# Edge counts kept as node by source tile: a bank evicted in one run, seven source tiles widened at once, eight gather buffers

## The chip, the core and the metric

The kernel runs on one core of one Trainium2 chip. Its engines work side by side, each through its own instructions in order, and wait for one another by semaphores: PE (TensorE, matrix products; its weight loads are shown as PEld), DVE (VectorE), ACT (ScalarE), POOL (GpSimd, which here issues the gathers and scatters) and SP (which issues plain DMAs). The metric is the device time of one execution in microseconds (us), the median of several runs.

## What is computed

One graph block over 6250 nodes with 256 features and 200,000 edges sorted by destination: a normalised input, a graph convolution plus a linear attention block, both added to the input, and then a mixture of 8 experts. The part that the change touches is the sum over edges in the graph convolution:

```python
edge_index = jnp.stack([src, dst])
xn = _layernorm(x, axis=-1)
x = x + gnn(edge_index, xn, W, b) + mix(xn, ...)
...
# in gnn, with self-loops appended to src and dst:
deg = segment_sum(ones, dst)
dinv = rsqrt(deg)
norm = dinv[src] * dinv[dst]
h = X @ W
out = relu(segment_sum(h[src] * norm[:, None], dst) + b)
```

The kernel sums the scaled rows of X over the edges of each node first, and multiplies by W behind it.

## The kernel before, in words

Nodes are handled in 49 tiles of 128 (`NB` = 49). The program has three stages. Up to about 273 us it searches the edge list, builds per-tile lists and scales the rows of X into `tab` (high and low part of each row side by side, 512 columns; all 49 tiles stay in SBUF as `source(t)` and are copied to `g_dram`). From 273 to about 1352 us runs the graph stage. Then the 8 experts run to the end.

**The graph stage** is three generators that are stepped in turn while the program is built (lines 1281 to 1302), so that each engine's order of instructions is fixed by that interleaving, under a manual schedule. One pass of the outer loop is one step of `gather`; `dense` is stepped as often as keeps it in proportion, `NGT + LAG` passes for `(ND + 1) * NS + 1` steps; `rounds` is stepped 1.25 times.

- **`gather`** (L971 to L998) serves 18 of the 49 destination tiles. Each of 612 passes issues an indirect DMA on POOL that fetches 128 rows of `g_dram` into a tile `gt` (L977), and, `LAG` = 7 passes later, multiplies the tile of seven passes ago by a one-hot matrix `oh` into PSUM (L995). `gt` has `GB` = 9 buffers.
- **`dense`** (L914 to L969) serves the other 31 destination tiles (`ND` = 31). For a destination tile `u` it builds a matrix of edge counts A and multiplies it with the source tiles. The 128 nodes are taken as 64 pairs, 5 pairs to a step, 13 steps (`NS` = 13, index `p`; the last step has 4 pairs). In a step DVE makes one-hot matrices `lo` (source row within its tile, 128 wide) and `hi` (98 wide: source tile and which node of the pair; L899); PE multiplies them pair by pair into one PSUM bank `bp` (L963), 98 columns for each pair; ACT copies the bank as bytes into `A` (L965). Before the change a pair's 98 columns are ordered by source tile, then node (`hi` = 2 x source tile + node, made at L592), and `A` lies as source tile by node, `[P, 49, 128]`. A bank of 10 nodes therefore goes to 245 places of `A`: 2 adjacent bytes, 128 bytes apart.
- The products with the source tiles come one destination tile later: while tile `u` is being counted, PE multiplies the counts of tile `u - 1`. Step `p` (1 to 12) takes 4 source tiles (the last one 5): `share(p)`. Before it, ACT widens those 4 slabs of bytes to 4-byte numbers in `A_r` (`widened`, L926, 512 elements per partition, or 640; 2 buffers); then PE does one 128x512 matmul per source tile into `ps_d` (L952). `make(k + 2)` lets DVE make the one-hots two steps ahead.
- **`rounds`** (L1083 to L1279) carries finished pairs of tiles on: attention, two layer norms, a two-layer MLP, gate and routing. It uses all engines; the lines that matter below are the normalisation on ACT from statistics of DVE (`nb` L1193, `s` and `slot` L1199), the transposes on PE that follow (L242), `agt` L1134, `x1t` L1213, `xmt` L1222, `ht` L1235 on ACT, the softmax of the routing with its ACT table load (L1025) and the scatter on POOL (L1076).

In one dense step the order is: PE's products L952 of step `p`; DVE's one-hots of step `p + 2`; ACT's widening for step `p + 1`; PE's counting L963; ACT's eviction L965. Since ACT works in order, a widening stands behind the eviction of the step before and behind whatever `rounds` put there.

Of the kernel before, what the change touches and what calls it, by code (L numbers as in the profile page):

```python
# [10 lines left out]
U8 = mybir.dt.uint8  # L11
FR = mybir.dt.float32r
AF = mybir.ActivationFunctionType
OP = mybir.AluOpType
# [4 lines left out]
P = 128  # L19
# [3 lines left out]
NB = 49  # L23
# [16 lines left out]
ND = len(DTS)  # L40
GN = 2
NG = P // GN
HI = NB * GN
NDC = (ND + 3) // 4
LS = 5
NS = (NG + LS - 1) // LS
# [2 lines left out]
NGT = NGB * EB  # L49
NGC = (NGT + P - 1) // P  # L50
IC = 64
GB = 9
LAG = 7
AHEAD = 4
SIDE = 1.25
NX = 6
# [13 lines left out]
def graph_block_kernel(  # L70
# [5 lines left out]
    nc = tc.nc  # L76
    V = nc.vector
# [39 lines left out]
    def table(t):  # L117

        k = t // 8
        if k not in tabs:  # L120
            where = (3, 4, 5, 0, 1, 2, 6)[k]
            tabs[k] = big.tile([P, min(8, NB - 8 * k), 2 * D], FR, name="tab", tag=f"T{where}")
            if k == NB // 8:
                V.tensor_copy(tabs[k][:, 0, :].rearrange("p (h d) -> p h d", h=2),
                              zeros.unsqueeze(1).to_broadcast([P, 2, D]))
        return tabs[k], t - 8 * k
# [5 lines left out]
    def source(t):  # L132
        o, at = table(t)
        return o[:, at, :]
# [368 lines left out]
    def edge_lists():  # L503
# [19 lines left out]
        for k, v in enumerate((begin_d, pid_d)):  # L523
            o = sm_ps[:, 128 + 32 * k:128 + 32 * k + 2 * NDC]
# [17 lines left out]
        def ask(c):  # L542
            if c < NGC:
                got[c] = [rw.tile([P, P], I32, name=o, tag=o) for o in ("gd", "gs")]
                fetch(got[c], gsi[:, c:c + 1])
            elif c < NGC + NDC:
                d = 2 * (c - NGC)
                got[c] = [rw.tile([P, 2, P], I32, name=o, tag=o) for o in ("wd", "ws")]
                for h in range(2):
                    fetch([w[:, h, :] for w in got[c]], ei[:, d + h:d + h + 1])  # L550
# [28 lines left out]
        for c in range(NDC):  # L579
            wd, ws = got.pop(NGC + c)  # L580
            hs = rw.tile([P, 2, P], I32, name="hs", tag="hs")
            kf = wd.bitcast(F32)
            for h in range(2):
                V.tensor_scalar(kf[:, h, :], wd[:, h, :], node0[:, 2 * c + h:2 * c + h + 1], None, op0=OP.subtract)
            vl = rw.tile([P, 2, P], F32, name="vl", tag="vl", bufs=1)
            V.tensor_scalar(vl, kf, 0.0, None, op0=OP.is_ge)
            V.scalar_tensor_tensor(vl, kf, float(GN), vl, op0=OP.is_lt, op1=OP.mult)
            V.tensor_copy(vend[:, 2 * c:2 * c + 2], vl[:, :, P - 1])
            yield
            V.tensor_scalar(hs, ws, 7, None, op0=OP.arith_shift_right)  # L590
            V.tensor_scalar(ws, ws, P - 1, None, op0=OP.bitwise_and)
            V.scalar_tensor_tensor(kf, hs, float(GN), kf, op0=OP.mult, op1=OP.add)  # L592
            yield
            V.scalar_tensor_tensor(kf, kf, -200.0, vl, op0=OP.add, op1=OP.mult)
            V.tensor_scalar(kf, kf, 200.0, None, op0=OP.add)
            lf = hs.bitcast(F32)
            V.tensor_copy(lf, ws)
            yield
            for v, o in ((kf, hiT), (lf, loT)):
                et_ps = rps.tile([P, 512], F32, name="et_ps", tag="et_ps", bufs=2)  # L600
                for h in range(2):
                    nc.tensor.transpose(et_ps[:, h * P:(h + 1) * P], v[:, h, :], ident)
                nc.scalar.copy(o[:, 4 * c:4 * c + 4, :].rearrange("p b g -> p (b g)"), et_ps[:, :2 * P])
            ask(NGC + c + 2)
            yield
# [264 lines left out]

    with tc.tile_pool(name="ga", bufs=GB, side="right") as ga, \
            tc.tile_pool(name="de", bufs=2, side="right") as de, \
# [9 lines left out]
        def put_sum(t, ps):  # L882
            gi = t // 2
            if gi not in sums:
                sums[gi] = pair("G", 3, "ag")
            V.tensor_reduce(sums[gi][:, t % 2, :], ps.rearrange("p (h d) -> p d h", h=2), AX.X, OP.add)
            there.add(t)

        def groups(p):
            return LS * p, min(NG, LS * (p + 1))  # L890

        def onehots(lists, p):

            o = []
            g0, g1 = groups(p)
            for name, row, w, t in (("lo", rowb, P, lists[0]), ("hi", hib, HI, lists[1])):
                one = de.tile([P, LS, w], BF16, name=name, tag=name, bufs=3)
                full = [P, g1 - g0, w // 2, 2]
                V.tensor_tensor(one[:, :g1 - g0, :].rearrange("p g (w t) -> p g w t", t=2),  # L899
                                row.rearrange("p (w t) -> p w t", t=2).unsqueeze(1).to_broadcast(full),  # L900
                                t[:, g0:g1, :].unsqueeze(2).to_broadcast(full), op=OP.is_equal)
                o.append(one)
            return o

        def twice(u):

            o = []
            for name, t in (("lo2", loT), ("hi2", hiT)):
                two = de.tile([P, NG, 2], BF16, name=name, tag=name)
                nc.scalar.copy(two, t[:, u, :].unsqueeze(2).to_broadcast([P, NG, 2]))  # L910
                o.append(two)
            return o

        def dense():  # L914

            mats, parts = {}, {}
            acc_ps = None

            def share(p):
                return (p - 1) * NB // (NS - 1), p * NB // (NS - 1)  # L920

            def widened(u, p):

                s0, s1 = share(p)
                o = parts[p] = de.tile([P, 5, P], FR, name="A_r", tag="A_r")
                nc.scalar.copy(o[:, :s1 - s0, :], mats[u][:, s0:s1, :])  # L926

            steps = [(u, p) for u in range(ND) for p in range(NS)]
            twos_ = {0: twice(0)}
            made = {}  # L930

            def make(k):
                if k < len(steps):
                    u, p = steps[k]
                    made[k] = onehots(twos_[u], p)
                    if p == NS // 2 and u + 1 < ND:
                        twos_[u + 1] = twice(u + 1)

            make(0)
            make(1)  # L940
            yield
            for u in range(ND + 1):
                for p in range(NS):
                    k = u * NS + p
                    if u >= 1 and p >= 1:

                        if p == 1:
                            acc_ps = dps.tile([P, 2 * D], F32, name="ps_d", tag="ps_d")
                            nc.tensor.matmul(acc_ps, identr, source(DTS[u - 1]), start=True, stop=False)
                        A, (s0, s1) = parts.pop(p), share(p)  # L950
                        for hi in range(s0, s1):
                            nc.tensor.matmul(acc_ps, A[:, hi - s0, :], source(hi), start=False, stop=(hi == NB - 1))  # L952
                    make(k + 2)
                    if u < ND and p == 0:
                        mats[u] = de.tile([P, NB, P], U8, name="A", tag="A")
                    if u >= 1 and p < NS - 1:
                        widened(u - 1, p + 1)
                    if u < ND:
                        lo, hi = made.pop(k)
                        g0, g1 = groups(p)  # L960
                        bp = bps.tile([P, 512], F32, name="bp", tag="bp")
                        for g in range(g1 - g0):
                            nc.tensor.matmul(bp[:, g * HI:(g + 1) * HI], lo[:, g, :], hi[:, g, :],  # L963
                                             start=(g == 0), stop=(g == g1 - g0 - 1))
                        nc.scalar.copy(mats[u][:, :, GN * g0:GN * g1].rearrange("p s (g k) -> p g s k", k=GN),  # L965
                                       bp[:, :(g1 - g0) * HI].rearrange("p (g s k) -> p g s k", g=g1 - g0, k=GN))
                    if u >= 1 and p == NS - 1:
                        put_sum(DTS[u - 1], acc_ps)
                    yield  # L969

        def gather():  # L971
            tiles, ohs = {}, {}
            ps = None
            for j in range(NGT + LAG):
                if j < NGT:
# [4 lines left out]
                    if j % IC == IC - 1:  # L980
                        sources(j // IC + 2)
                i = j - LAG
                m = i + AHEAD
# [310 lines left out]
        while any(alive.values()):  # L1294
            step("g", G)
            while alive["d"] and done_d * (NGT + LAG) < n_dense * (j + 1):
                step("d", Dn)
# [146 lines left out]
```

## Time and profile before

| | |
|---|---|
| median of 4 runs | 1726.28 us (1724.23 to 1734.5) |
| the profiled execution | 1726.21 us, its span on the core 1724.3 us |
| busy over the span | PE 1463.2 us, ACT 1110.3, DVE 1084.5, POOL 781.5 |
| L965, evictions of the counts | 403, 513.1 us, mean 1276 ns |
| L926, widening of the counts | 372, 252.0 us, mean 678 ns |
| L952, products with source tiles | 1519, mean 420 ns |
| L977, gathers on POOL | 612, mean 1030 ns |

Times in the views are microseconds, and means of one instruction are in nanoseconds. Matmuls overlap one another in the array, so a group of four lasts less than four times its mean. An engine's "busy" leaves out waiting. A wait is put down to the instruction that released it.

### The profile page before, as it was taken

Reading aid. Unit: us, or ns where it says so; the run is one execution under the profiler, and the core shown is the slowest. Engines: PE = TensorE matmul, PEld = TensorE weight load, DVE = VectorE, ACT = ScalarE, POOL = GpSimd, SP = SyncE. Lnnn points to the kernel's source line nnn. Section 1 sums busy time; section 2 is a strip of 40 time slices with the busy share of each in tenths; the row PEclk is TensorE's granted clock in tenths of the full one; section 3 lists DMA queues with packets and bytes.
Section 4 is the critical chain, followed back from the end, with each engine's and each line's share of the span. In section 5 each row is a group of like instructions: output and inputs, shape, how many; then the busy total and the mean of one; then the engine's idle time right before and its main releaser. Section 6 shows DMA issues by size and latency. Waiting matters only on the chain. (4 is left out here: it accounts for less than half of the span.)

```text
span 1724.3 us, 23628 instructions
## 1 busy us (share of the span) xinstructions
PE 1463.2 (85%) x7678; PEld 1043.3 (61%) x7678; DVE 1084.5 (63%) x3430; ACT 1110.3 (64%) x1794; POOL 781.5 (45%) x771
## 2 busy tenths in 40 slices
PE   4888785999978988798898888888898479999997
PEld 1555554666656666576666566656666256777775
DVE  5766867877777787667876777777776313233232
ACT  1755666878877887688778777878787123333332
POOL 0103605757556665655666556647675201111101
PEclk9988997999989998999989999999999789999999
DMA  7536886768566766665766566757675533333330
GB/s 224 175 103 177 279 296 183 206 164 205 152 176 177 188 171 186 169 173 157 198 165 182 157 168 173 198 145 191 161 206 147 185 111 116 115 110 113 114 107 22
DMA packets 184987, 286.42 MB, mean 166 GB/s; under 512 B 28458, under 2 KB 78565, under 8 KB 184715
## 3 DMA queue, kind: packets, MB, share of 16 engines
q0 software_dynamic: 96304, 180.15, 40.0%
q1 hardware_dynamic: 88250, 103.44, 18.3%
q8 instruction: 69, 1.13, 0.3%
q10 hardware_dynamic: 288, 1.08, 0.2%
q14 instruction: 76, 0.61, 0.1%
HBM read 226.90 MB, written 60.39 MB: 167 GB/s over the span
## 5 line engine op out<-in xcount | busy, mean ns | idle before, releaser
L977 POOL DMA_INDIRECT gt<-g_dram,idxc x612 | 630.5, 1030 | 423.2 <-PE ps L995 228.9
L965 ACT CAST A<-bp 128x490 uint8<-128x490 f32 (+1 forms) x403 | 513.1, 1276 | 147.7 <-PE bp L963 146.2
L952 PE MATMUL ps_d<-tab,A_r 128*128 128x512 f32 x1519 | 448.6, 420 | 48.8 <-ACT A_r L926 47.8
L952 PEld LDWEIGHTS ps_d<-tab,A_r 128*128 128x128 f32 x1519 | 285.1, 197 | 143.9 <-ACT A_r L926 88.2
L995 PE MATMUL ps<-gt,oh 128*128 128x512 f32 x612 | 274.9, 483 | 8.6 <-DMA gt<-g_dram,idxc 4.8
L926 ACT CAST A_r<-A 128x512 fp32r<-128x512 uint8 x372 | 252.0, 678 | 9.3 <-PE ps_d L952 8.5
L899 DVE TENSOR_TENSOR lo<-rowb,lo 128x640 bf16<-128x640 bf16 (+1 forms) x403 | 193.8, 481 | 59.9 <-PE bp L963 49.6
L963 PEld LDWEIGHTS <-lo 128*128 128x128 bf16 x1984 | 105.4, 102 | 130.4 <-issue 43.3
L963 PE MATMUL bp<-hi,lo 128*128 128x98 bf16 x1984 | 165.7, 215 | 16.3 <-DVE hi L899 15.9
L1388 POOL DMA_INDIRECT out<-rep,who x43 | 42.4, 985 | 300.4 <-DVE rep L1386 202.0
L899 DVE TENSOR_TENSOR hi<-hib,hi 128x490 bf16<-128x490 bf16 (+1 forms) x403 | 162.6, 404 | 0.0
L986 DVE TENSOR_TENSOR oh<-rowb,rel 128x256 fp32r<-128x256 bf16 x306 | 127.5, 417 | 49.6 <-PE ps L995 49.3
L1360 PE MATMUL hpf<-xet,w1e 128*128 128x512 f32 (+2 forms) x544 | 151.6, 436 | 5.6 <-ACTq L1400 3.5
L1370 PE MATMUL ypf<-w2e,hm 128*128 128x256 f32 (+1 forms) x688 | 151.3, 379 | 0.0
L1370 PEld LDWEIGHTS ypf<-w2e,hm 128*128 128x128 f32 (+1 forms) x688 | 128.9, 188 | 21.9 <-issue 3.4
L1360 PEld LDWEIGHTS hpf<-xet,w1e 128*128 128x128 f32 x544 | 85.7, 192 | 65.3 <-issue 57.4
L1362 ACT ACTIVATE hm<-hpf,fb_s 128x512 f32<-128x512 f32 (+2 forms) x136 | 71.0, 525 | 78.4 <-PE hpf L1360 74.0
L995 PEld LDWEIGHTS ps<-gt,oh 128*128 128x128 f32 x612 | 111.8, 198 | 15.6 <-DMA gt<-g_dram,idxc 6.3
L1372 DVE TENSOR_TENSOR y<-ypf,fb_s 128x256 f32<-128x256 f32 (+1 forms) x43 | 18.2, 423 | 141.4 <-PE ypf L1370 141.4
L1373 ACT ACTIVATE y<-y,xe 128x256 f32<-128x256 f32 (+1 forms) x43 | 21.9, 508 | 119.3 <-DVE y L1372 119.3
L721 PE MATMUL mm<-wqkv_s,xnt 128*128 128x512 f32 (+1 forms) x196 | 97.7, 623 | 0.0
L1199 ACT ACTIVATE s<-s,nb,rs 128x256 f32<-128x256 f32 (+1 forms) x98 | 53.5, 594 | 50.9 <-DVE nb L1193 50.9
(307 smaller groups left out, 2028.6 us busy)
## 6 DMA issues: line engine op xcount, KB each, us to landing
g_dram<-tab SPq DMA_DIRECT2D x24, 512.0 KB, 4.6
xt<-in_x SPq DMA_DIRECT2D x42, 256.0 KB, 5.4
xbuf<-zeros SPq DMA_DIRECT2D x26, 384.0 KB, 4.6
gt<-g_dram,idxc POOLq DMA_INDIRECT x612
xe<-xbuf SPq DMA_DIRECT2D x8, 1028.0 KB, 6.4
w1e<-in_fw SPq DMA_DIRECT2D x8, 1024.0 KB, 4.7
w2e<-in_fw SPq DMA_DIRECT2D x8, 1024.0 KB, 5.3
xe<-xbuf SPq DMA_DIRECT2D x8, 771.0 KB, 10.2
```

Of the source, the lines that this page charges most:

```text
L721: nc.tensor.matmul(kp[:r, :], xnt[:, c, i * r:i * r + r], wqkv_s[:, c, D:3 * D], start=(c == 0), stop=(c == 1))
L899: V.tensor_tensor(one[:, :g1 - g0, :].rearrange("p g (w t) -> p g w t", t=2), row.rearrange("p (w t) -> p w t", t=2).unsqueeze(1).to_broad ...
L926: nc.scalar.copy(o[:, :s1 - s0, :], mats[u][:, s0:s1, :])
L952: nc.tensor.matmul(acc_ps, A[:, hi - s0, :], source(hi), start=False, stop=(hi == NB - 1))
L963: nc.tensor.matmul(bp[:, g * HI:(g + 1) * HI], lo[:, g, :], hi[:, g, :], start=(g == 0), stop=(g == g1 - g0 - 1))
L965: nc.scalar.copy(mats[u][:, :, GN * g0:GN * g1].rearrange("p s (g k) -> p g s k", k=GN), bp[:, :(g1 - g0) * HI].rearrange("p (g s k) -> p ...
L977: nc.gpsimd.indirect_dma_start(out=gt, out_offset=None, in_=g_dram, in_offset=bass.IndirectOffsetOnAxis(ap=idxs[j // IC][:, j % IC:j % IC ...
L986: V.tensor_tensor(oh, rowb.unsqueeze(1).to_broadcast([P, 2, P]), rel[:, m:m + 2].unsqueeze(2).to_broadcast([P, 2, P]), op=OP.is_equal)
L995: nc.tensor.matmul(ps, ohs.pop(i), tiles.pop(i), start=False, stop=(e == EB - 1))
L1360: nc.tensor.matmul(hp[:, :nn], w1e[:, c, f * P:(f + 1) * P], xet[:, c, at:at + nn], start=(c == 0), stop=(c == 1))
L1362: nc.scalar.activation(hm[:, f, :nn], hp[:, :nn], AF.Relu, bias=fb1_s[:, e * 8 + f:e * 8 + f + 1])
L1370: nc.tensor.matmul(yp[:r, :], hm[:, f, (i - i0) * P:(i - i0) * P + r], w2e[:, f, :], start=(f == 0), stop=(f == DFF // P - 1))
```

## The change

`A` is laid out as node by source tile, `[P, 128, 49]`; `hi` becomes 49 x node + source tile, so that a pair's 98 columns in PSUM have the same order and a bank of 10 nodes is 490 consecutive bytes of `A`. The widening then takes 7 source tiles at once (`CH` = 7, 7 pieces for each destination tile in place of 12), and reads for each of the 7 source tiles 128 bytes that lie 49 bytes apart. A piece is asked for when PE's products start on the piece before it; the first piece behind the last eviction of its tile, the second in step 0 of the next. `A_r` has still 2 buffers, of 7 x 128 numbers in place of 5 x 128. `gt` has 8 buffers in place of 9 and `LAG` is 6 in place of 7.

```diff
-GB = 9
-LAG = 7
+GB = 8
+LAG = 6
...
-            V.scalar_tensor_tensor(kf, hs, float(GN), kf, op0=OP.mult, op1=OP.add)
+            V.scalar_tensor_tensor(kf, kf, float(NB), hs, op0=OP.mult, op1=OP.add)
...
+            CH = 7
...
-            def widened(u, p):
-                s0, s1 = share(p)
-                o = parts[p] = de.tile([P, 5, P], FR, name="A_r", tag="A_r")
-                nc.scalar.copy(o[:, :s1 - s0, :], mats[u][:, s0:s1, :])
+            def widened(u, c):
+                if 0 <= u < ND and c * CH < NB:
+                    o = parts[u, c] = de.tile([P, CH, P], FR, name="A_r", tag="A_r")
+                    nc.scalar.copy(o, mats[u][:, :, c * CH:(c + 1) * CH].rearrange("p n s -> p s n"))
...
-                        A, (s0, s1) = parts.pop(p), share(p)
-                        for hi in range(s0, s1):
-                            nc.tensor.matmul(acc_ps, A[:, hi - s0, :], source(hi), start=False, stop=(hi == NB - 1))
+                        for hi in range(*share(p)):
+                            nc.tensor.matmul(acc_ps, parts[u - 1, hi // CH][:, hi % CH, :], source(hi),
+                                             start=False, stop=(hi == NB - 1))
                     make(k + 2)
                     if u < ND and p == 0:
-                        mats[u] = de.tile([P, NB, P], U8, name="A", tag="A")
-                    if u >= 1 and p < NS - 1:
-                        widened(u - 1, p + 1)
+                        mats[u] = de.tile([P, P, NB], U8, name="A", tag="A")
+                    if p >= 1:
+                        for hi in range(*share(p)):
+                            if hi and hi % CH == 0:
+                                widened(u - 1, hi // CH + 1)
...
-                        nc.scalar.copy(mats[u][:, :, GN * g0:GN * g1].rearrange("p s (g k) -> p g s k", k=GN),
-                                       bp[:, :(g1 - g0) * HI].rearrange("p (g s k) -> p g s k", g=g1 - g0, k=GN))
+                        nc.scalar.copy(mats[u][:, GN * g0:GN * g1, :].rearrange("p n s -> p (n s)"), bp[:, :(g1 - g0) * HI])
+                    if p == NS - 1:
+                        widened(u, 0)
+                    if p == 0:
+                        widened(u - 1, 1)
```

## The prediction

> **What bounds the kernel now.** I read the busy time by stretches first, then the waits, the groups with shapes kept apart, and the timeline around the longest waits. The counting, the widening and the gathers all run between 273 and 1352 us:
>
> ```profile
> core 0: us, PE busy (x) PEld busy (x) DVE busy (x) ACT busy (x) POOL busy (x), PEclk, DMA share, GB/s
> 273.00:1352.00 1079.00, 936.70 (x5466) 680.10 (x5465) 798.99 (x2515) 857.09 (x1211) 678.61 (x656) 0.94 0.67 177
> 740.00:760.00 20.00, 20.00 (x126) 14.59 (x125) 15.13 (x40) 17.93 (x24) 13.17 (x13) 1.00 0.65 160
> 500.00:520.00 20.00, 13.49 (x75) 9.78 (x74) 15.31 (x48) 13.85 (x22) 8.76 (x9) 0.83 0.55 146
> ```
>
> No engine is full, but PE comes closest: it is idle for 1079 - 937 = 142 us. Whatever the change gives must come out of these, or out of PE's clock. So the question is which of PE's waits end on ACT:
>
> ```profile
> ACT A L965 <- PE bp L963: 146.2, 94, 4.1
> PEld ps_d L952 <- ACT A_r L926: 88.2, 136, 6.6
> ACT s L1199 <- DVE nb L1193: 50.9, 24, 4.8
> PE ps_d L952 <- ACT A_r L926: 47.8, 46, 6.3
> PE ps L995 <- DMA gt<-g_dram,idxc: 4.8, 8, 1.2
> PE mm L242 <- ACT s L1199: 37.8, 29, 3.4
> PE mm L1161 <- ACT agt L1134: 9.5, 12, 2.3
> ```
>
> PE loses 47.8 us to a late widening, and ACT itself waits 146 us for PE's counts: ACT is not the bound on the average, but late at certain places. The timeline shows two kinds of place:
>
> ```profile
> 801.80 1.28 ACT L1025 ACT_TABLE_LOAD   x1
> 803.23 0.71 ACT L926 CAST A_r<-A 128x640 fp32r<-128x640 uint8 x1
> 803.99 1.44 PE L952 MATMUL ps_d<-tab,A_r 128*128 128x512 f32 x5 [1.63 <-ACT A_r L926]
> ...
> 731.23 1.09 ACT L1199 ACTIVATE s<-s,nb,rs 128x256 f32<-128x256 f32 x2 [3.17 <-DVE nb L1193]
> 733.21 0.60 ACT L926 CAST A_r<-A 128x512 fp32r<-128x512 uint8 x1
> 733.86 1.65 PE L952 MATMUL ps_d<-tab,A_r 128*128 128x512 f32 x3 [5.16 <-ACT A_r L926]
> ```
>
> In the first, ACT worked through an eviction and a table load ahead of the widening: ACT was busy, and cheaper evictions help. There are seven such waits, 11.0 us in all. In the second, ACT stood at the normalisation until DVE had `nb`, with the widening queued behind it. Five such waits (2.56, 6.30, 5.16, 4.89, 4.86) are 23.8 of the 47.8 us, and a cheaper eviction does not shorten them.
>
> **The eviction.** Before, it writes 245 runs of 2 bytes, 128 bytes apart; after, 490 bytes in one run. The rows:
>
> ```profile
> L965 ACT CAST A<-bp 128x490 uint8<-128x490 f32 x372 | 480.8, 1295 | 124.2 <-PE bp L963 122.8 <-issue 0.4
> L926 ACT CAST A_r<-A 128x512 fp32r<-128x512 uint8 x341 | 228.1, 669 | 9.3 <-PE ps_d L952 8.5
> L926 ACT CAST A_r<-A 128x640 fp32r<-128x640 uint8 x31 | 24.0, 773 | 0.0
> L603 ACT CAST loT<-et_ps 128x256 uint8<-128x256 f32 x8 | 3.1, 388 | 0.0
> L573 ACT CAST rel<-et_ps 128x512 bf16<-128x512 f32 x1 | 0.6, 619 | 0.0
> L428 DVE CAST lastf<-dl 125x25 f32<-125x25 int32 x1 | 0.2, 185 | 0.0
> L477 DVE TENSOR_SCALAR cnt<-cnt 112x24 f32<-112x24 f32 x1 | 0.2, 175 | 0.0
> ```
>
> From PSUM into one run of bytes, 256 elements take 388 ns (L603); from PSUM, 512 take 619 ns (L573). That is 0.90 ns an element, so 490 take 599 and 392 take 511. Saved: 372 x (1295 - 599) = 259 us, and 31 x (1050 - 511) = 17 us (1050 is the mean of the 128x392 form); 276 us of ACT's work.
>
> **The widening.** If a read pays nothing for its step of 49 bytes, the two forms of L926 give (773 - 669) / 128 = 0.81 ns an element on a base of 253, so 896 elements take 981 ns; 217 of them 213 us in place of 252: 39 us less. No row shows ACT reading single bytes far apart, so the price has two ends. The low end is 981 ns. At the high end a read costs what a write in the same pattern costs: (1295 - 253) / 245 = 4.25 ns a run, so 253 + 896 x 4.25 = 4.06 us; counted by element instead (2.13 ns), 2.16 us. The nearest row of a read is DVE's L428: 25 numbers 256 bytes apart in 185 ns, against 175 ns for 24 numbers 8 bytes apart (L477), at most 0.4 ns an element more. I take the low end, since that row is a read, and ACT would then need 1.34 us at most.
>
> A rule speaks against the change here. The Trainium skill (page "SBUF — State Buffer", section on SBUF as two separate sides) says that SBUF works in 16-byte lines and that a line must be hit twice for the access to be hidden, so bytes may lie 16 apart and no more for free. A step of 49 never hits a line twice; if that doubles the time per element, a widening takes about 1.7 us as an estimate and the sum below would be some 1715. L428 breaks the same rule without such a price.
>
> **What comes off the path.** ACT's busy time in the stage falls to 857 - 276 - 39 = 542 us. PE's stream changes by no matmul. Counted one by one:
> - The other 24.0 us of the 47.8: I take 20, since fewer widenings (217 for 372) are asked for one to two steps ahead instead of one, behind evictions that are 0.7 us shorter.
> - The 23.8 us behind `nb`: the lead lets a third of them pass; 8 us.
> - PEld's wait is 40 us longer than PE's, in some 90 places of mostly 0.25 us. There the array still streams; in the one that I followed (823.48) the products started 0.09 us late. 90 x 0.08 = 7 us.
> - `agt` 9.5, `ht` 3.6, `x1t` 1.1, `xmt` 1.8 us: one eviction stands before most of them; half, 8 us.
> - The transposes behind `s` and `slot` (37.8 + 6.3): ACT itself waits 58.7 us for DVE's `nb` there; nothing.
> - The clock: 0.83 in the stretch with a wait of 6.3 us, 1.00 in the one without idle. Scaled by idle time, 40 us less of 142 would be worth 14 us of the 937; but the long waits stay, so I take 4.
>
> Sum 47 us. The Trainium skill ("TensorE: Matmul & The Clock Gate", Part 1) has the clock halve only after a whole idle window of about 3.4 us; by that rule the waits that go are all too short and the 4 us would be 0.
>
> **What is given back.** Widening piece 0 is ordered behind the last eviction of its tile: 511 + 981 ns against 1050 + 669 before, nothing lost. Later pieces wait in ACT's queue until PE has left the buffer; behind them stand only that step's eviction, whose counts PE makes later anyway, and `rounds`. A piece is ordered 7 matmuls ahead: 7 x 0.233 (spacing of L952: four in 1.09 with the first 0.39) plus 1.75 steps of counting (0.22) and 1.5 gather products (0.34) is 2.6 us; so a widening below about 2 us is hidden. The fewer buffers: each gather still waits for a matmul issued two passes earlier; it has eight passes instead of nine until its use, about 1.75 us less of a median 7.6 us between its start and its product. PE and PEld wait 11.1 us for gathers now. A gather keeps POOL 0.94 + 0.30 us; a dense step without `rounds` streams in 1.66 us and wants 1.47 gathers, 1.13 us each, so POOL becomes the slower one there: I take 8 us more. DVE, 799 us busy plus some 0.04 us between its 2515 instructions, is 900 us taken, and its one-hots (15.9 us of waits for `hi`) and its chain to the routing (23.0) will be waited for longer: 5 us. The edit at L592 swaps two operands, 8 times in the first stage: nothing.
>
> Together 47 - 13 = 34 us: 1726.2 - 34 = **1692 us** (the profiled run, 1726.21, is the median within 0.1).
>
> **The rivals.**
> - *The strided read is priced like the strided write* (slower). Place: L926; it decides from about 2.1 us a widening, where it no longer fits the 2.6 us lead and each of 31 tile starts loses 1.2 us, 37 us, all of the gain. At 2.16 us: about 1729. At 4.06: ACT has 857 - 276 - 252 + 882 = 1211 us in a stage of 1079, and with its 58.7 us of waits for `nb` the stage takes 1270: 1917 us. For it: the eviction shows such bytes to be dear. Against: a write of part of a word is another matter than a read, and L428. 18%.
> - *The read is slowed halfway*: 1.47 ns an element, 1.57 us. Hidden except at tile starts, 31 x 0.6 = 18 us: 1710. 20%.
> - *ACT's relief is taken over by others*: the freed time comes back as waits for DVE and POOL (900 and 612 x 1.24 + 48 x 1.39 = 826 us taken of 1079): 1722 to 1728. For it: ACT's own idle time of 146 us. Against: the seven waits behind a table load have nothing else late. 14%.
> - *All waits for ACT go*: 47.8 + 7 + 16 + 44, and half of the clock's deficit, 29 us, less the 13: 1595. Against: `nb` is DVE's. 8%.
>
> **How the numbers follow.** The forecast has 40%, with a range of its own of 1660 to 1712. Below 1635 I leave half of the last rival; above 1745 most of the first. Less than 0.5% (8.6 us) can't be told from no change. Faster: 40 + 8, 14 of the halfway case and 2 of the takeover, 64%; same: 6 + 8, 14%; slower: 18 + 4, 22%.
>
> **What would show it.** Evictions near 600 ns; widenings near 981 ns (1.6 or 2.2 and more: the rivals); waits for `A_r` down to some 15 us, the long ones behind `nb` still there; waits on `gt` near 20 us; ACT near 540 us in the stage. I am wrong if the widening takes over 2 us, or if ACT falls to 540 and PE's idle time stays near 140.

## The result, and the profile after

Nothing was gained and nothing lost: 1730.48 us median (1722.42 to 1737.75, 44 runs) against 1730.36 us (1719.98 to 1736.36, 70 runs) for the kernel before, a ratio of 1.0006 with a 95% interval of 0.9997 to 1.0016. The forecast was 1692 us, faster by 2%.

The profiled execution of the changed kernel has a span of 1733.8 us. It is 9.5 us longer than the one shown of before, while the medians agree; so differences of a few us between single lines of the two profiles mean little.

First the groups of ACT, shapes kept apart (busy us, mean ns of one | idle before, and what ended it):

```profile
L927 ACT CAST A_r<-A 128x896 fp32r<-128x896 uint8 x217 | 392.8, 1811 | 71.0 <-PE ps_d L952 69.1 <-ACT A L969 0.3
L969 ACT CAST A<-bp 128x490 uint8<-128x490 f32 x372 | 205.7, 570 | 107.7 <-PE bp L967 106.8
```

The eviction fell from 1295 to 570 ns, a little under the forecast 599. The widening did not cost the 981 ns that I took but 1811 ns: together 393 us in place of 252. Per element, with the 1349 ns of 640 elements from experiment e8 below, it is (1811 - 1349) / 256 = 1.80 ns, against 0.81 ns before.

Then the waits of PE (total us, times, longest):

```profile
PE mm L242 <- ACT s L1206: 51.8, 27, 4.3
PE mm L1056 <- DVE fore L1052: 33.0, 12, 4.4
PE bp L967 <- DVE hi L899: 20.1, 7, 9.0
PE mm L1168 <- ACT agt L1141: 13.9, 12, 2.2
PE ps L1002 <- DMA gt<-g_dram,idxc: 11.1, 15, 2.5
PE mm L1238 <- ACT x1t L1220: 10.7, 7, 2.4
PE ps_d L952 <- ACT A_r L927: 3.3, 5, 1.1
```

These lines show why PE idles as long as before. The wait for `A_r` went from 47.8 to 3.3 us: the change did remove it. But `s` went from 37.8 to 51.8 us, `fore` from 23.0 to 33.0, the gathers from 4.8 to 11.1, `x1t` from 1.1 to 10.7, `agt` from 9.5 to 13.9, `hi` from 15.9 to 20.1: 14.0 + 10.0 + 6.3 + 9.6 + 4.4 + 4.2 = 48.5 us come in, 44.5 us go out. The lines alone do not say which part of the change brought which wait; experiment e3 does. The stretch of the graph stage shows the same (the columns are those of the prediction's first view):

```profile
273.00:1352.00 1079.00, 938.01 (x5446) 701.48 (x5447) 798.47 (x2510) 785.56 (x1057) 673.96 (x656) 0.91 0.66 176
```

PE is idle for 141 us of the 1079, as before. ACT has 786 us, where 542 were forecast.

The timeline shows how `x1t` came to be late:

```profile
484.05 1.76 ACT L927 CAST A_r<-A 128x896 fp32r<-128x896 uint8 x1
485.71 1.03 ACT L969 CAST A<-bp 128x490 uint8<-128x490 f32 x2
486.63 1.02 ACT L1220 ACTIVATE x1t<-mm,be_c,g_c 128x256 f32<-128x256 f32 x2
487.25 2.07 PE L1238 MATMUL mm<-x1t,w_s 128*128 128x256 f32 x4 [2.15 <-ACT x1t L1220]
```

A widening of 1.76 us and two evictions stand before `x1t` in ACT's queue, and PE waits 2.15 us. (Shortly before, ACT had stood for 3.79 us at `s` until DVE had `nb`, and it was working off what had queued up.) The products that the widening serves do not wait for it; the MLP of `rounds` does.

### The profile page after: what moved, and what is told of

The parts are those of the page before. It is cut to its first block, busy times and chain, and to the rows that moved or that the text cites. A ratio compares the mean times of both kernels' runs of the same rounds, so it can differ in the third digit from the quotient of the medians.

```text
span 1733.8 us, 23596 instructions
## 1 busy us (share of the span) xinstructions
PE 1473.3 (85%) x7678; PEld 1070.6 (62%) x7678; DVE 1086.2 (63%) x3430; ACT 1039.5 (60%) x1639; POOL 776.5 (45%) x771
## 5 line engine op out<-in xcount | busy, mean ns | idle before, releaser
L952 PE MATMUL ps_d<-tab,A_r 128*128 128x512 f32 x1519 | 441.4, 416 | 3.4 <-ACT A_r L927 3.3
L927 ACT CAST A_r<-A 128x896 fp32r<-128x896 uint8 x217 | 392.8, 1811 | 71.0 <-PE ps_d L952 69.1
L952 PEld LDWEIGHTS ps_d<-tab,A_r 128*128 128x128 f32 x1519 | 305.4, 201 | 72.4 <-ACT A_r L927 7.3
L969 ACT CAST A<-bp 128x490 uint8<-128x490 f32 (+1 forms) x403 | 220.7, 563 | 148.8 <-PE bp L967 147.8
L1002 PE MATMUL ps<-gt,oh 128*128 128x512 f32 x612 | 282.3, 495 | 11.5 <-DMA gt<-g_dram,idxc 11.1
L967 PE MATMUL bp<-hi,lo 128*128 128x98 bf16 x1984 | 167.3, 216 | 20.1 <-DVE hi L899 20.1
L1002 PEld LDWEIGHTS ps<-gt,oh 128*128 128x128 f32 x612 | 115.7, 204 | 20.3 <-DMA gt<-g_dram,idxc 10.8
L1206 ACT ACTIVATE s<-s,nb,rs 128x256 f32<-128x256 f32 (+1 forms) x98 | 53.5, 594 | 61.1 <-DVE nb L1200 61.1
```

The source lines that it names most:

```text
L927: nc.scalar.copy(o, mats[u][:, :, c * CH:(c + 1) * CH].rearrange("p n s -> p s n"))
L952: nc.tensor.matmul(acc_ps, parts[u - 1, hi // CH][:, hi % CH, :], source(hi), start=False, stop=(hi == NB - 1))
L969: nc.scalar.copy(mats[u][:, GN * g0:GN * g1, :].rearrange("p n s -> p (n s)"), bp[:, :(g1 - g0) * HI])
L1002: nc.tensor.matmul(ps, ohs.pop(i), tiles.pop(i), start=False, stop=(e == EB - 1))
```

## The experiments

After the result there were two explanations for the missing gain. The first, called takeover in the expectations: ACT's load in the counting is not what sets the end, and whatever it frees comes back as waits in `rounds`. The second: the gain is there, and the strided read ate it. A third put it on the ring of gather buffers. The first four runs tell these apart.

**e1, the ring alone.** The kernel before with

```diff
-GB = 9
-LAG = 7
+GB = 8
+LAG = 6
```

> The kernel before with 8 gather buffers and a lag of 6 alone. Theory (takeover): the widening's waits went, and other links of the graph stage that are just as tight became the ones that end last; the ring plays no part: 1730 us, within 5. Rival (the ring ate the gain): with one buffer fewer PE waits longer for gathers, and this alone costs what the layout brought, 25 to 40 us: 1755 to 1770.

Measured: 1741.95 us against 1732.8 of the kernel before on the same chip, ratio 1.0056 (1.0034 to 1.0079). The lines of this run that moved, waits for gathers:

```profile
PEld ps L995 <- DMA gt<-g_dram,idxc: 15.3, 17, 2.6
PE ps L995 <- DMA gt<-g_dram,idxc: 15.0, 18, 2.3
```

6.3 and 4.8 us before. Both expectations missed: the ring does cost something, some 10 us, but not the whole gain.

**e3, a cheap widening in the changed kernel.** It reads the same number of bytes in one run. The counts then meet the wrong source tiles, so the sums over edges are other ones; the work is the same in number and size.

```diff
-                    nc.scalar.copy(o, mats[u][:, :, c * CH:(c + 1) * CH].rearrange("p n s -> p s n"))
+                    flat = mats[u].rearrange("p n s -> p (n s)")
+                    nc.scalar.copy(o.rearrange("p s n -> p (s n)"), flat[:, c * CH * P:(c + 1) * CH * P])
```

> The changed kernel with its widening reading 896 consecutive bytes instead of 7 x 128 bytes at a step of 49; the counts then meet the wrong source tiles, so the sums over edges are not the reference's; the work is the same in number and size. The widening should take some 0.98 us instead of 1.81, 180 us less of ACT. Theory (takeover): ACT's load is not what sets the end; 1715 to 1730. Rival (the price of the strided read ate the gain): the gain of the prediction appears, about 1695.

Measured: 1694.42 us, ratio 0.9793 (0.9764 to 0.9821). Its ACT rows:

```profile
L970 ACT CAST A<-bp 128x490 uint8<-128x490 f32 x372 | 210.0, 565 | 211.3 <-PE bp L968 210.2
L928 ACT CAST A_r<-A 128x896 fp32r<-128x896 uint8 x217 | 204.3, 942 | 93.1 <-PE ps_d L953 91.8
```

With the widening at 942 ns the forecast's 1692 us are there, ring and all. Takeover, which I held, falls; the step of the read decides.

Its stage, cut as close to its end as the row of the changed kernel above, and the waits of PE to set beside those above:

```profile
273.00:1312.00 1039.00, 916.77 (x5437) 687.87 (x5438) 796.73 (x2505) 604.24 (x1054) 671.15 (x655) 0.93 0.70 183
PE mm L242 <- ACT s L1207: 50.7, 26, 4.3
PE mm L1057 <- DVE fore L1053: 30.0, 12, 4.4
PE mm L1239 <- ACT x1t L1221: 5.5, 5, 1.7
PE mm L1169 <- ACT agt L1142: 4.9, 8, 1.0
```

`s` and `fore` stay almost as long as in the changed kernel, `hi` too (19.1 us), and the waits for gathers grow to 17.4 us. So none of these came with the price of the read. Nor does the ring alone bring `s` and `fore` up (39.6 and 23.6 us in e1), nor a cheap eviction alone (35.0 and 22.3 in e4): they seem to come with the new order and size of the widenings. What the cheap read takes away is `x1t`, `agt` and `ht` (4.4 us in the changed kernel, 1.0 here): together 29.0 us fall to 11.4, about as much as the 19 us by which PE's idle time falls (141 to 122). The other half of the 40 us is PE's busy time, 938 to 917 us, at a granted clock of 0.93 in place of 0.91. Why PE is busy for less is not shown. The two profiled executions lie 44 us apart and the medians 36, so some of it is spread.

**e4, the eviction in another order, nothing else.** The kernel before; the bank is walked by source tile and then by its 10 nodes, so that 49 runs of 10 bytes are written, and the widening stays contiguous:

```diff
-                        nc.scalar.copy(mats[u][:, :, GN * g0:GN * g1].rearrange("p s (g k) -> p g s k", k=GN),
-                                       bp[:, :(g1 - g0) * HI].rearrange("p (g s k) -> p g s k", g=g1 - g0, k=GN))
+                        nc.scalar.copy(mats[u][:, :, GN * g0:GN * g1].rearrange("p s (g k) -> p s g k", k=GN),
+                                       bp[:, :(g1 - g0) * HI].rearrange("p (g s k) -> p s g k", g=g1 - g0, k=GN))
```

> The kernel before, only the order in which an eviction walks the bank changed: source tile, then the 10 nodes, so that it writes 49 runs of 10 bytes instead of 245 runs of 2, and the widening stays contiguous at 0.67 us. If a run costs 4.25 ns, the eviction falls to some 0.7 us; ACT 240 us less. Theory (takeover): 1715 to 1730 although ACT has little left. Rival (price of the strided read): 1690 to 1700.

Measured: 1691.03 us, ratio 0.9773 (0.9738 to 0.9808); it beats both kernels.

```profile
L965 ACT CAST A<-bp 128x490 uint8<-128x490 f32 x372 | 219.9, 591 | 261.5 <-PE bp L963 260.5 <-issue 0.2
L926 ACT CAST A_r<-A 128x512 fp32r<-128x512 uint8 x341 | 211.1, 619 | 10.6 <-PE ps_d L952 9.8
```

Runs of 10 bytes are written nearly as fast as one run of 490 (591 and 570 ns). The step did not vanish: the bank is now read in PSUM by pairs of numbers, 98 numbers (392 bytes) apart, where the kernel before read it in one run. That is in the 591 ns, so there it costs at most 21 ns. The widening, whose instruction is unchanged, fell as well, from 669 to 619 ns.

**e5, room between the links of `rounds`** in the kernel before:

```diff
-SIDE = 1.25
+SIDE = 1.5
...
                 V.scalar_tensor_tensor(nb, mstat[:, :, 0], -1.0, rs, op0=OP.mult, op1=OP.mult)
+                yield
+                yield
                 yield
                 yield
...
                     norm(slot[:, :, :D], slot[:, :, D:2 * D], cr, cn, 4)
+                yield
                 yield
                 yield
...
                     nc.scalar.copy(agt[:, :, :cn * cr], tp[:, :, :cn * cr])
+                yield
                 yield
...
                     norm(ss[b], ss[b], br, bn, 2)
                 yield
+                yield
...
                 V.tensor_add(fore[:, b + 1, :], fore[:, b, :], oh[:, b, :])
+            yield
+            yield
             yield
             yield
```

> The kernel before with more room between the links of the rounds: two more steps between DVE's nb and the normalisation on ACT, one between the normalisation and its transposes, one behind agt, one ahead of the products with x1t, two behind fore; the rounds stepped 1.5 times a pass instead of 1.25. Theory (takeover, the links of the rounds stall PE and ACT in their queues): waits of PE for s and fore shrink and the time falls by 15 to 50 us, 1680 to 1715. Rival (ACT's load in the counting is what counts): 1725 to 1735.

Measured: 1700.12 us, ratio 0.981 (0.9765 to 0.9854). Its waits:

```profile
PE ps_d L952 <- ACT A_r L926: 60.4, 60, 4.2
PE mm L242 <- ACT s L1204: 6.3, 9, 1.9
PE mm L1051 <- DVE fore L1045: 5.5, 4, 4.4
```

`s` falls from 37.8 to 6.3 us and `fore` from 23.0 to 5.5. So the links of `rounds` do cost time, as takeover said; but e3 and e4 show that ACT's dear instructions cost it as well. They are two causes.

**e6 and e7, the same room in the changed kernel and in e4.**

> The changed kernel with the same extra room between the links of the rounds as e5. New theory (price and ring: the widening's 1.81 us in place of 0.98 took 36 us back, one buffer fewer some 10). If the widening's price acts through the rounds, whose operations on ACT stand behind a widening of 1.8 us (waits for s, x1t, agt), room takes that away: 1680 to 1690, more than the 32 us of e5. If it acts through ACT's load alone, room brings the same 32 us as in e5: about 1698.

> e4 (runs of 10 bytes, contiguous widening) with the room of e5. If late evictions and tight links are two causes, their gains add: 1691 - 32 = 1659. If they are the same waits counted twice: 1680 to 1690.

e6: 1697.35 us, ratio 0.9808 (0.9753 to 0.9863). e7: 1660.17 us, ratio 0.9589 (0.9538 to 0.964). Room brings 33 us in the changed kernel and 31 us on top of e4, what it brings in the kernel before: the gains add. e7 is the fastest of this study measured beside the kernel before at 1732 us. That room would help most where a widening takes 1.8 us did not come true. e6 came out at the 1698 us that were expected if the price acts through ACT's load alone, not at the 1680 to 1690 of a price that acts through `rounds`. This speaks against the reading of e3's waits, but does not settle it: in e6 waits for `fore` (21.6 us), `agt` (11.6) and `A_r` (9.6) remain, so the room did not free all that is held up.

**e8, the ring back, pieces of 5.** The changed kernel with

```diff
-GB = 8
-LAG = 6
+GB = 9
+LAG = 7
...
-            CH = 7
+            CH = 5
...
-                    nc.scalar.copy(o, mats[u][:, :, c * CH:(c + 1) * CH].rearrange("p n s -> p s n"))
+                    w = min(CH, NB - c * CH)
+                    nc.scalar.copy(o[:, :w, :], mats[u][:, :, c * CH:c * CH + w].rearrange("p n s -> p s n"))
```

> The changed kernel with its 9 gather buffers and lag of 7 back; for the room in SBUF it widens 5 source tiles at once (10 pieces a tile instead of 7, 93 more bases of 0.25 us). Theory (price and ring): the 10 us of e1 come back, a few are lost to the pieces: 1720 to 1727. Rival (the ring costs nothing once the layout is changed): 1730 to 1737.

Measured: 1715.72 us, ratio 0.9916 (0.9888 to 0.9943), more than expected although ACT works longer (411 us of widening for 393):

```profile
L928 ACT CAST A_r<-A 128x640 fp32r<-128x640 uint8 x279 | 376.2, 1349 | 70.1 <-PE ps_d L953 66.5
L928 ACT CAST A_r<-A 128x512 fp32r<-128x512 uint8 x31 | 34.4, 1108 | 0.0
```

**e9, the price on the other side.** The changed kernel; the widening reads 128 runs of 7 adjacent bytes and writes numbers of 4 bytes 512 bytes apart:

```diff
-                    nc.scalar.copy(o, mats[u][:, :, c * CH:(c + 1) * CH].rearrange("p n s -> p s n"))
+                    nc.scalar.copy(o.rearrange("p s n -> p n s"), mats[u][:, :, c * CH:(c + 1) * CH])
```

> The changed kernel, only the order in which a widening walks its 896 numbers changed: node, then source tile, so that it reads 128 runs of 7 adjacent bytes and writes numbers of 4 bytes 512 bytes apart. If the 1.81 us is the price of reads that are alone in their line, the widening falls to about 1.0 us and the kernel to about 1695. If any access out of line costs the same, read or write: 1.8 us, 1730. If a write out of line costs what the eviction's runs cost (4.25 ns each): 4 us, 1900.

Measured: 1724.35 us, ratio 0.9964 (0.9938 to 0.999).

```profile
L927 ACT CAST A_r<-A 128x896 fp32r<-128x896 uint8 x217 | 388.4, 1791 | 73.3 <-PE ps_d L952 71.1 <-ACT A L969 0.3
```

Numbers written one by one far apart, with their reads in runs of 7, cost what bytes read one by one far apart cost. Turning this loop round only moves the step from one side to the other.

**e10, e12 and e13: ring and pieces apart; e11: more room.** e10 is e8 with 8 buffers and a lag of 6; e11 is e7 with about double the room (`SIDE` 1.75). They fell on a chip on which the kernel before takes 1859 us, so only ratios compare; e12 and e13 are e8 and e10 again, side by side there.

> e8 with 8 gather buffers and a lag of 6, as the changed kernel has: pieces of 5 source tiles instead of 7 alone. ACT works 20 to 25 us more than in the changed kernel, but never for more than 1.35 us at a stretch in a widening (1.81 there). If the length of one widening counts beside the sum of them (rounds' operations wait behind it): 1722 to 1727, and the ring's share in e8's gain is some 10 us as in e1. If only ACT's load counts: 1732 to 1737, and the ring was worth 16 to 20 us in this layout.

> e7 with about double the room between the links of the rounds, stepped 1.75 times a pass. If e7 has taken all that the links cost: 1655 to 1665, or longer at the end, where the rounds finish later. If links still stall PE (nb 43 us of ACT's idle time, A_r 37, fore 6): 1640 to 1652.

> e8 once more, beside e10 on one chip (e10 and e11 ran on a chip on which the kernel before took 1859 us). As e8: 0.992 of the kernel before.

> e10 once more, beside e12. If the ring costs in this layout what it cost in e1 (0.56%), 0.997 to 0.998 of the kernel before, and pieces of 5 instead of 7 are worth the rest to 1.0006, some 0.3%. If pieces of 5 are worth nothing or lose, 1.000 or more.

e10: 0.9939 (0.9908 to 0.9969). e12, 9 buffers: 0.9926 (0.9897 to 0.9955). e13, 8 buffers: 0.9963 (0.9932 to 0.9994). The changed kernel, with 8 buffers and pieces of 7, has 1.0006 over all its runs, but none of these was on that chip, where other waits lead: PE waits 69.3 us for `A_r` in e12 and 14.4 in e8, the same kernel. So the 0.4 to 0.7% between them are a hint that pieces of 5 pay although they add work, not a proof. On the faster chips e8 is 15 us under the changed kernel, of which e1 gives the ring 10; what is left is within the intervals. That the length of one widening counts beside the sum is not shown. The ring between e12 and e13 is about 0.4%, with intervals that overlap; e1's 0.56% is the clearer figure. e11: 0.9685 (0.9628 to 0.9743), worse than e7's ratio, but on the other chip, so it isn't settled whether more room than e7's helps or harms.

## Why the prediction was wrong

**The step that failed** is the price of the widening, "I take the low end": 981 ns taken, 1811 measured. It was mis-sized by 0.83 us x 217 = 180 us of ACT's work; e3, which takes (1811 - 942) x 217 = 189 us of it away, is 36 us faster than the changed kernel.

**The rest of the sum** holds in its total: with the read contiguous (e3, 942 ns) the kernel takes 1694 us where the sum had 1692. That is luck in part, for its terms do not hold. From 273 us to the last gather product, PE's idle time falls by 19 us from the kernel before to e3 (141 to 122), where the sum, without the clock, had 43 - 13 = 30; PE's busy time falls by 16 us (935.8 to 919.5), where 4 us stood for the clock.

**Why I took the low end.** I let DVE's 25 numbers at 256 bytes decide, "since that row is a read". It was another engine, another width and one instruction of 185 ns, too short to show what 25 steps cost. The rule that I set against it (the Trainium skill, "SBUF — State Buffer", the section on the two separate sides: 16-byte lines, two hits needed) fits ACT's read here: 1.7 us as an estimate, with the doubling that I assumed, and 1.81 measured.

**The halfway rival** had the right mechanism and too low a price: 1.57 us and 1710. Even at 1.81 us its own account, 31 tile starts x 0.83 = 26 us, leads to 1718, not to 1730. The sentence behind it, "a widening below about 2 us is hidden", is true only of the products that need it: `A_r` is waited for 3.3 us. It is not hidden from `rounds`, whose operations stand behind it on ACT: the timeline at 484 us shows one case, and the waits for `x1t`, `agt` and `ht`, 29.0 us that are 11.4 in e3, show the sum; only e6 speaks against it. I named what stands behind the widening ("that step's eviction ... and `rounds`") and priced `rounds` at nothing.

**The takeover rival** had the right time, measured against the kernel before (1722 to 1728 us beside 1726, 14%), for a reason that the runs refute as the whole cause: ACT's relief pays once it is real: e3 is 36 us faster than the changed kernel, e4 42 us faster than the kernel before. A part of it is true: waits for `s`, `fore`, `hi` and gathers do take the place of those for `A_r`, in e3 too.

**The signs of being wrong** did not come as written: the widening stayed under 2 us, and PE's idle time stayed at 141 us without ACT falling to 540.

**The other terms.** Evictions: 599 ns forecast, 570 measured. The 24 us of `A_r` waits behind busy ACT went, and so did the 23.8 us behind `nb`, of which I let only a third pass (3.3 us are left of both); but that stall seems to have come back one link on, as the 14.0 us more for `s`, which I had put at nothing: ACT still stands 61.1 us at `s` for DVE's `nb`, 50.9 before. DVE: 5 us taken, while the waits for `hi` and `fore` rose by 14 us, and by 10 in e3. The ring: 8 us taken, about 10 measured (e1), and the waits for gathers are 11.1 + 10.8 us after, near the 20 forecast. The reasoning behind it had a wrong figure, the 7.6 us median between a gather and its product: with each of the 612 gathers set beside its own product it is about 12.3 us before and 10.7 after, 1.6 us less where I took 1.75. `agt`, `ht` and `x1t` were to fall and rose. The clock was to rise with less idle time: it is 0.91 in the stage after and 0.94 before, at the same idle time, and 0.93 in e3 with 122 us of idle time in its stage of 1039 us; idle time alone doesn't set it. Nor were the waits that went all short, as I wrote: the longest for `A_r` was 6.3 us before and is 1.1 after, and the clock fell all the same. Over whole runs the medians are 0.92 after and 0.94 before, so this is more than one profile's chance.

**What stays open:** how the 36 us of the dear widening divide between its length and its sum; why about half of them are PE's busy time and not its waits; and how far room in `rounds` can go.

## What to carry to other kernels

A layout that makes one side of a transposed copy contiguous moves the step to the other side; price both sides by rows of the same engine and the same width, and if there is none, take the dear end. Look first for a loop order of the same copy that puts the step where it is cheap (e4: runs of ten bytes written, pairs of numbers read from PSUM, 21 ns more than with no step); it changes no layout. In a queue that works in order a long instruction can be charged to what stands behind it more than to the one who waits for its result: here 29.0 us for `x1t`, `agt` and `ht` against 3.3 for `A_r`.

## What the runs showed of the hardware

On ACT, 49 runs of 10 bytes are written in 591 ns and one run of 490 in 570, but 245 runs of 2 bytes in 1295: (1295 - 570) / 245 = 3.0 ns more for each run. The 591 ns include a read of PSUM by 245 pairs of numbers 392 bytes apart. Single bytes read 49 bytes apart cost 1.80 ns each for 0.81 in a row; single 4-byte numbers written 512 bytes apart, from reads in runs of 7, come to the same (1791 ns for 896). The rule of two hits in a line, named above, fits the last two; the runs of 2 bytes hit their line twice and are dear nevertheless, which it does not explain.

An instruction's time can depend on its neighbours: the widening of 512 bytes in one run takes 669 ns beside the dear eviction (before, e1, e5) and 618 to 619 beside the cheap one of e4, e7 and e11. Why is not shown.

Chips differ: the kernel before took 1732 us on one and 1859 us on another. The widenings of 640 bytes took the same time on both (1349 and 1342 ns in e8 and e12). From 273 us to the last gather product e12 takes 126 us more than e8: PE idles 217 us in place of 135 and is busy 972 in place of 928, at a granted clock of 0.89 in place of 0.93. So most of it is waiting.
